# Turning the gathered rows of ten of eleven routed tiles by way of memory and VectorE's block transposes

## The chip, the core and the metric

The kernel runs on one core of a Trainium2 chip. The metric is the device time of one execution in microseconds (us), as the median of several runs. TensorE (PE in the profile), VectorE (DVE), ScalarE (ACT), GpSimd (POOL) and SyncE (SP) each work through their own instructions in order; SP here only issues DMAs.

## What is computed

The input is 625 rows of 1024 numbers and a graph of 20000 edges. A graph layer (normalise, per relation a projection and a mean over the edges, ELU, an output projection, a residual) gives x1. A mixture-of-experts layer follows, on h = layernorm(x1):

```python
sh = gelu(h @ sW1[s] + sb1[s]);  shared = mean_s(sh @ sW2[s] + sb2[s])
w  = softmax over the two largest of (h @ rW + rb), zero elsewhere
moe = sum_e w[:, e] * (gelu(h @ W1[e] + b1[e]) @ W2[e] + b2[e])      # 8 experts, 1024 -> 256 -> 1024
out = x1 + shared + moe
```

All of it is in float32. The change lies in the routed part, `gelu(h @ W1[e] + b1[e])` for the two experts that each row is routed to.

## The kernel before

**Order of the work.** A graph part, then the shared experts' first layer (`shared_in`, 32 groups of matmuls into p_sh), beside which VectorE works out the routing: which row sits in which slot of which tile (`tok`), and which expert each tile or part of a tile belongs to (`ej`, read into registers by TensorE and ScalarE). Then the routed first layer, the routed second layer (`p_yj`, whose rows are scattered to memory `yt`), the shared second layer (`p_o`) with the gathered sums, and the store.

**The routed tiles.** There are NJ = 11 tiles of 128 slots. Seven belong to one expert each, three are shared by two experts (64 slots each), one by four (32 each). Their order of work is the tuple `tiles`: 4, 5, 6, 0, 7, 1, 8, 2, 9, 10, 3. The text counts tiles in this order of work.

**The stages before the change.** `fetch` (L1368) gathers the tile's rows from memory `h2d` by an indirect DMA from GpSimd into `xs` (128 x 1024), of which there are three buffers in pool `io`; the bias rows `b2x` use the same three. TensorE then turns the rows: eight transposes of 128 x 128 into two PSUM banks (`p_x`, L1378), of which ScalarE copies the first to `xsT` (L1384) and VectorE the second (L1382). `xsT` has two buffers. `expert_in` (L1397) multiplies `xsT` with the expert's W1 into `p_h` (8 steps of 128 features), VectorE copies that to `hj` (L1401). `expert_mid` (L1409) turns `hj` by TensorE into `p_hT`, and ScalarE applies the GELU into `hjT` (L1412). The loop runs these three one step apart: fetch with turn of tile s, `expert_in` of s - 1, `expert_mid` of s - 2. For tiles with more than one expert, ScalarE copies the further experts' W1 to a fixed place (`w1m`, L1391), at set steps.

**What sets the order.** The program text is scheduled: each engine gets a fixed list of instructions, not always in the order of the text, and works through it in order. A DMA waits, in its engine's queue, for what it needs, and with it all behind it. SP's queue before the change, from the middle on: `yt` zeroed, W1 of two experts, both shared sW1, W1 of six experts, W2 of all eight experts (L1109, 1 MB each, into `w2a`), then (waiting for the last `p_h`) sW2 and the rows of x1, later the loads `g` from `yt` and the stores. `w2a` holds all eight experts' W2; the second layer picks from it by a register, so that its first matmul waits for all eight.

**Feature order.** W1 is loaded as `(k p) h -> p k h`: partition p holds features p, 128 + p, and so on, in runs of 1 KB, which fits the order in which the transposes lay the features out.

## Time and profile before

| | |
|---|---|
| median of 3 runs | 295.31 us (295.11 to 295.79) |
| the profiled execution | 294.8 us |
| its span, first to last instruction | 293.0 us |
| TensorE busy | 283.4 us (97%) |
| VectorE, ScalarE, GpSimd busy | 168.3, 103.2, 44.1 us |
| shared first layer ends | 161.1 us |
| routed first layer, first turn to first p_yj | 161.1 to 212.1 us |
| turns of the rows, p_x | 88 matmuls, 0.87 us for the eight of a tile |
| W1 loads issued | 94.0 to 129.9 us |
| W2 loads issued | 133.3 to 144.2 us |

The page has six parts: busy time by engine, the span in 40 slices, the DMA queues, the chain that ended last (followed back from the last instruction to whatever released each step), the costliest groups of instructions, and the DMA issues. Beside it stand answers of the trace: the chain in order of time, timelines of one engine (start, length, engine, line, operation, output and inputs, count, and in brackets the idle time before it with what ended it), and busy time by window. `PEld` is TensorE's loading of weights, and a name such as `ACTq` is an engine's queue, where register loads and waits are seen. A float32 matmul shows as two records, a transpose as one.

### The profile page before, as it was taken

Reading aid. Unit: us, or ns where it says so; the run is one execution under the profiler, and the core shown is the slowest. Engines: PE = TensorE matmul, PEld = TensorE weight load, DVE = VectorE, ACT = ScalarE, POOL = GpSimd, SP = SyncE. Lnnn points to the kernel's source line nnn. Section 1 sums busy time; section 2 is a strip of 40 time slices with the busy share of each in tenths; the row PEclk is TensorE's granted clock in tenths of the full one; section 3 lists DMA queues with packets and bytes.
Section 4 is the critical chain, followed back from the end, with each engine's and each line's share of the span. In section 5 each row is a group of like instructions: output and inputs, shape, how many; then the busy total and the mean of one; then the engine's idle time right before and its main releaser. Section 6 shows DMA issues by size and latency. Waiting matters only on the chain.

```text
span 293.0 us, 4532 instructions
## 1 busy us (share of the span) xinstructions
PE 283.4 (97%) x1573; PEld 192.1 (66%) x1573; DVE 168.3 (57%) x459; ACT 103.2 (35%) x237; POOL 44.1 (15%) x101
## 2 busy tenths in 40 slices
PE   7998999999999999899999999999999999999992
PEld 5876777778888555677777987778643334444451
DVE  5699999997874888746925322222134111157920
ACT  2348425513642323353105544656198111000000
POOL 9500000000000024420131312110012223200000
PEclk9999999999999999999999999999999999999998
DMA  6999930000000999999999742420095545389351
GB/s 229 344 322 408 408 117 2 2 1 2 0 0 4 327 364 392 393 392 369 409 353 408 283 143 78 140 74 0 2 342 230 211 194 226 136 332 403 134 156 53
DMA packets 28699, 61.41 MB, mean 210 GB/s; under 512 B 2150, under 2 KB 15981, under 8 KB 28666
## 3 DMA queue, kind: packets, MB, share of 16 engines
q1 hardware_dynamic: 23144, 44.17, 42.0%
q0 software_dynamic: 5232, 16.55, 15.4%
q10 hardware_dynamic: 296, 0.35, 0.5%
q8 instruction: 15, 0.25, 0.3%
q14 instruction: 12, 0.10, 0.1%
HBM read 43.02 MB, written 18.81 MB: 211 GB/s over the span
## 4 chain that ended last, share of the span: by engine, by line
PE 77%; DVE 20%; issue 1%; ACT 1%; ACTq 0%; DVEq 0%
PE p_h L1397 13%; PE p_yj L1455 13%; PE p_o L1510 12%; PE p_sh L1175 11%; PE p_pr L920 9%; PE p_agg L937 5%; PE p_x L1378 3%; DVE ohs L873 3%; DVE ohs L874 2%; PE p_y L983 2%; PE scrap L1000 2%; DVE xh L987 2%; DVE st L776 2%; DVE xh L807 1%; DVE ohk L877 1%; DVE h L747 1%
## 5 line engine op out<-in xcount | busy, mean ns | idle before, releaser
L920 PE MATMUL p_pr<-wg,nT 128*125 128x286 f32 x240 | 61.5, 409 | 1.0 <-ACT nT L825 0.8
L920 PEld LDWEIGHTS p_pr<-wg,nT 128*125 128x125 f32 x240 | 43.8, 187 | 13.2 <-ACT nT L825 1.8
L1397 PE MATMUL p_h<-w1a,xsT 128*128 (+2 forms) x176 | 40.0, 381 | 0.0
L1455 PE MATMUL p_yj<-w2a,hjT 128*128 (+2 forms) x88 | 38.6, 595 | 0.0
L1510 PE MATMUL p_o<-sw,shT 128*125 128x512 f32 (+1 forms) x88 | 36.1, 554 | 0.0
L1175 PE MATMUL p_sh<-h2T,sw 128*128 128x313 f32 (+1 forms) x128 | 35.2, 429 | 0.0
L1397 PEld LDWEIGHTS p_h<-w1a,xsT 128*128 128x128 f32 (+2 forms) x176 | 28.8, 169 | 7.4 <-issue 0.5
L1175 PEld LDWEIGHTS p_sh<-h2T,sw 128*128 128x128 f32 x128 | 23.7, 190 | 8.6 <-issue 0.2
L1455 PEld LDWEIGHTS p_yj<-w2a,hjT 128*128 128x128 f32 (+2 forms) x88 | 14.4, 169 | 22.4 <-issue 22.4
L1510 PEld LDWEIGHTS p_o<-sw,shT 128*125 128x125 f32 x88 | 16.4, 188 | 16.9 <-issue 16.2
L1459 DVE COPY ys<-p_yj 128x512 f32<-128x512 f32 x15 | 10.4, 692 | 28.7 <-PE p_yj L1455 27.0
L1401 DVE COPY hj<-p_h 128x256 f32<-128x256 f32 x11 | 4.7, 425 | 31.1 <-PE p_h L1397 31.1
L994 POOL DMA_DIRECT2D x1d<-xh x10 | 5.3, 531 | 92.4 <-DVE flagf L721 89.0
L983 PE MATMUL p_y<-wo_t,eT 128*125 128x512 f32 (+1 forms) x40 | 18.8, 592 | 0.0
L1463 POOL DMA_INDIRECT yt<-ys,row x11 | 10.8, 981 | 50.5 <-DVE ys L1459 50.5
L1412 ACT ACTIVATE hjT<-p_hT,vT 128x128 f32<-128x128 f32 (+2 forms) x34 | 8.7, 332 | 24.5 <-PE p_hT L1409 24.5
L1486 DVE SCALAR_TENSOR_TENSOR x<-p_o,x 125x512 f32<-125x512 f32 (+1 forms) x11 | 6.9, 639 | 16.3 <-PE p_o L1512 16.3
L1370 POOL DMA_INDIRECT xs<-h2d,tok x11 | 10.4, 948 | 34.5 <-PE p_x L1378 24.9
L937 PE MATMUL p_agg<-P,CT 125*125 125x288 f32 x100 | 15.5, 305 | 0.0
L1397 PE MATMUL p_h<-w1m,xsT 128*64 128x256 f32 (+1 forms) x96 | 14.7, 382 | 0.0
L1455 PE MATMUL p_yj<-w2m,hjT 128*64 128x512 f32 (+1 forms) x48 | 14.1, 595 | 0.0
L1382 DVE COPY xsT<-p_x 128x512 f32<-128x512 f32 x11 | 7.6, 692 | 11.0 <-PE p_x L1378 8.7
(309 smaller groups left out, 422.8 us busy)
## 6 DMA issues: line engine op xcount, KB each, us to landing
w1a<-in_L_ffn_W_dram SPq DMA_DIRECT2D x8, 1024.0 KB
w2a<-in_L_ffn_W_dram SPq DMA_DIRECT2D x8, 1024.0 KB
yt<-zero SPq DMA_DIRECT2D x2, 2560.0 KB
g<-yt SPq DMA_DIRECT2D x10, 512.0 KB
sw<-in_L_ffn_sW_dram SPq DMA_DIRECT2D x4, 1024.0 KB
x<-x1d SPq DMA_DIRECT2D x5, 500.0 KB
x1d<-xh POOLq DMA_DIRECT2D x5, 448.0 KB, 7.2
h2d<-h POOLq DMA_DIRECT2D x5, 448.0 KB, 6.8
```

Source lines behind the costliest of these rows:

```text
L873: nc.vector.tensor_tensor(os, row[:, None].to_broadcast(shape), key, op=ALU.is_equal)
L920: nc.tensor.matmul(p[:TP, :F], nT[:, k, m * TP : (m + 1) * TP], wg[:, k, r, :], start=(k == 0), stop=(k == KD - 1))
L937: nc.tensor.matmul(p[:TP, : F + 2], CT[:, m, at : at + TP], P[:, m, r, i], start=(m == 0 and i == 0), stop=(m == NT - 1 and i == 1))
L983: nc.tensor.matmul(ps[s][:TP, :], eT[:n, k, :], wo_t[:n, k, at], start=(k == 0), stop=False)
L1175: nc.tensor.matmul(p[:, : z - a], sw1[:, i, k, t * 128 : (t + 1) * 128], h2T[:, k, a:z], start=(k == 0), stop=(k == KD - 1))
L1370: nc.gpsimd.indirect_dma_start(out=xs, out_offset=None, in_=h2d, in_offset=bass.IndirectOffsetOnAxis(ap=tok[:, j : j + 1], axis=0))
L1378: nc.tensor.transpose(p[:, k * 128 : (k + 1) * 128], xs[:, at : at + 128], ident)
L1397: nc.tensor.matmul(p[a:b, :H], xsT[j][:, k, a:b], w1m[j, a][:, 0, k, :] if a else w1a[:, bass.ds(e, 1), k, :], start=(k == 0), stop=(k == ...
L1455: made = nc.tensor.matmul(p[a:b], hjT[:, j, k, a:b], w2m[j, a, k][:, at] if a else w2a[:, bass.ds(e, 1), k, at], start=(k == 0), stop=(k = ...
L1459: nc.vector.tensor_copy(y[:, at], p)
L1463: sent.append(nc.gpsimd.indirect_dma_start(out=yt, out_offset=bass.IndirectOffsetOnAxis(ap=row[:, j : j + 1], axis=0), in_=y, in_offset=No ...
L1510: nc.tensor.matmul(p[:TP, :n], shT[:, i, k, own], sw2[:, i, k, at], start=(i == 0 and k == 0), stop=False)
```

## The change

- Memory `xd` is added, 512 KB for each tile.
- For all tiles but the first, `fetch` also writes the gathered rows to `xd`, each row cut in four quarters of 256 features (a DMA on SP's queue).
- `turn` is one step later than the gather. For these ten tiles it reads `xd` back (again on SP's queue) such that partition 32b + r holds quarter b of rows 4r to 4r + 3. The landing place is one of two halves of the last expert's place in `w2a`. VectorE then turns blocks of 32 x 32 straight into `xsT`, in one instruction of 128 x 1024.
- The first tile is still turned by TensorE, taking every eighth column of `xs`.
- In `xsT`, partition p then holds features 8p to 8p + 7. So W1 is loaded as `(p k) h -> p k h`, one run of 8 KB for each partition.
- `w2a`: four experts are loaded where all eight were, three in the first steps of the loop, and the last one, into the landing place, after the last turn.
- `expert_in` and `expert_mid` come one step later, and the loop has one step more. The copies of `w1m` are ordered after the last GELU written ahead of them in place of the copy of `xsT`.

```diff
+    xd = dram.tile([NJ, 4, QC * D], F32, name="xd")
@@ load_w1
-            nc.sync.dma_start(w1a[:, e], W1[e].rearrange("(k p) h -> p k h", p=128))
+            nc.sync.dma_start(w1a[:, e], W1[e].rearrange("(p k) h -> p k h", p=128))
@@
-    for e in range(NE):
-        nc.sync.dma_start(w2a[:, e], W2[e].rearrange("(k p) d -> p k d", p=128))
+    def load_w2(es):
+        for e in es:
+            nc.sync.dma_start(w2a[:, e], W2[e].rearrange("(k p) d -> p k d", p=128))
+    load_w2(range(4))
@@ routed tiles
+    turned = [last_in]
+    fetched = {}
 
     def fetch(j):
         xs = io.tile([128, D], F32, tag="io", name=f"xs_{j}")
         nc.gpsimd.indirect_dma_start(
...
+        fetched[j] = xs
+        if j not in by_pe:
+            nc.sync.dma_start(xd[j].rearrange("b (n f) -> n b f", n=128), xs.rearrange("n (b f) -> n b f", b=4))
+
+    def through_blocks(s, t_):
+        j = tiles[s]
+        xq = w2a[:, NE - 1, s % HK].rearrange("p (a f) -> p a f", a=4)
+        nc.sync.dma_start(xq, xd[j].rearrange("b (r a f) -> (b r) a f", r=QC, a=4))
+        nc.vector.transpose(t_.rearrange("p k (r a) -> p a k r", a=4), xq.rearrange("p a (c k) -> p a k c", k=KD))
+
+    def turn(s):
+        j = tiles[s]
         t_ = xt.tile([128, KD, 128], F32, tag="xsT", name=f"xsT_{j}")
-        for g in range(2):
-            p = ps_acc(f"p_x{g}_{j}")
-            for k in range(4):
-                at = (4 * g + k) * 128
-                nc.tensor.transpose(p[:, k * 128 : (k + 1) * 128], xs[:, at : at + 128], ident)
...
+        if j in by_pe:
+            for g in range(2):
+                p = ps_acc(f"p_x{g}_{j}")
+                for k in range(4):
+                    nc.tensor.transpose(p[:, k * 128 : (k + 1) * 128], fetched[j][:, 4 * g + k :: KD], ident)
+                (nc.vector.tensor_copy if g else nc.scalar.copy)(
+                    t_[:, 4 * g : 4 * g + 4, :], p.rearrange("p (k n) -> p k n", k=4))
+        else:
+            through_blocks(s, t_)
         xsT[j] = t_
...
-            with tc.issue_after(copied.ins):
+            with tc.issue_after(turned[-1].ins):
@@ the loop
+    by_pe = [tiles[s] for s in (0,)]
-    for s in range(NJ + 2):
+    for s in range(NJ + 3):
         if s < NJ:
             fetch(tiles[s])
         if 0 <= s - 1 < NJ:
-            expert_in(tiles[s - 1])
+            turn(s - 1)
+        if 4 <= s + 4 - 1 < NE - 1 and s:
+            load_w2((s + 4 - 1,))
+        if s == NJ:
+            load_w2((NE - 1,))
         if 0 <= s - 2 < NJ:
-            expert_mid(tiles[s - 2])
+            expert_in(tiles[s - 2])
+        if 0 <= s - 3 < NJ:
+            expert_mid(tiles[s - 3])
```

More of the change, by code (lines that the diff above doesn't have):

```diff
@@ L1176, in shared_in @@
                                  h2T[:, k, a:z], start=(k == 0), stop=(k == KD - 1))
-            nc.scalar.activation(shT[:, i, t, a:z], p[:, : z - a], AF.Gelu, bias=vT[:, b : b + 1])
+            last = nc.scalar.activation(shT[:, i, t, a:z], p[:, : z - a], AF.Gelu, bias=vT[:, b : b + 1])
+        return last
     wab = const.tile([TP, 2, NT], F32, name="wab")
@@ L1345, in sparse_kernel @@
     for t in range(HK):
-        shared_in(1, t)
+        last_in = shared_in(1, t)
     sh_in.close()
@@ L1372, in fetch @@
             in_offset=bass.IndirectOffsetOnAxis(ap=tok[:, j : j + 1], axis=0))
-        t_ = xt.tile([128, KD, 128], F32, tag="xsT", name=f"xsT_{j}")
-        for g in range(2):
-            p = ps_acc(f"p_x{g}_{j}")
-            for k in range(4):
-                at = (4 * g + k) * 128
-                nc.tensor.transpose(p[:, k * 128 : (k + 1) * 128], xs[:, at : at + 128], ident)
-            o = t_[:, 4 * g : 4 * g + 4, :]
-            pv = p.rearrange("p (k n) -> p k n", k=4)
-            if g:
-                nc.vector.tensor_copy(o, pv)
-            else:
-                copied = nc.scalar.copy(o, pv)
+        fetched[j] = xs
[8 more added lines that the diff above has]
+        j = tiles[s]
+        t_ = xt.tile([128, KD, 128], F32, tag="xsT", name=f"xsT_{j}")
+        if j in by_pe:
[7 more added lines that the diff above has]
+            through_blocks(s, t_)
         xsT[j] = t_
@@ L1411, in expert_mid @@
             for a, b, e in parts(j):
-                nc.scalar.activation(hjT[:, j, t, a:b], p[:, t * 128 + a : t * 128 + b], AF.Gelu,
-                                     bias=bT[:, bass.ds(e, 1), t])
+                turned.append(nc.scalar.activation(hjT[:, j, t, a:b], p[:, t * 128 + a : t * 128 + b],
+                                                   AF.Gelu, bias=bT[:, bass.ds(e, 1), t]))
     whole = range(NM2, NJ)
```

## The prediction

> **What bounds the kernel now.** I read the page's busy shares first, then the chain that ended last around the changed stage, then the timelines of ScalarE and GpSimd there, then the DMA queues by window.

> ```profile
> PE 283.4 (97%) x1573; PEld 192.1 (66%) x1573; DVE 168.3 (57%) x459; ACT 103.2 (35%) x237; POOL 44.1 (15%) x101
> ```

> TensorE is the bound. In the routed stage the chain of work runs on TensorE alone:

> ```profile
> 161.14 1.75 PE p_x L1378 x16
> 162.88 3.46 PE p_h L1397 x16
> 166.34 0.87 PE p_x L1378 x8
> 167.21 3.46 PE p_h L1397 x16
> 170.67 0.22 PE p_hT L1409 x2
> 170.89 0.87 PE p_x L1378 x8
> ```

> Columns: start, length, work. Each tile pays 0.87 us for turning its rows (p_x) before 3.46 us of first-layer matmuls (p_h); the first two tiles' turns stand together. So work taken from TensorE here counts in full, if nothing later than TensorE comes up. The places where that can happen are the start and the end of the stage. At the start:

> ```profile
> 161.18 0.52 ACT L1177 ACTIVATE shT<-p_sh,vT 128x312 f32<-128x312 f32 x1 [1.68 <-PE p_sh L1175]
> 161.61 0.59 ACT L1384 COPY xsT<-p_x 128x512 f32<-128x512 f32 x1
> 162.54 0.59 ACT L1384 COPY xsT<-p_x 128x512 f32<-128x512 f32 x1 [0.34 <-PE p_x L1378]
> 164.39 2.18 ACT L1391 COPY w1m<-w1a 128x512 f32 x4 [1.26 <-DMA w2a<-in_L_ffn_W_dram]
> ```

> ```profile
> L1354 ACTq TENSOR_LOAD <-ej x1: 1452/1452/1452, 162.6 to 162.6; - x1
> ```

> ScalarE copies the first tiles' columns at once and only then does the register load and the four expert copies (w1m). The profile puts the wait of 1.26 us down to a DMA; the register load of 1.45 us in its queue fills that time better. The gathers:

> ```profile
> 147.18 1.04 POOL L1370 DMA_INDIRECT xs<-h2d,tok  x1 [0.32 <-DVE part L1330]
> 148.52 0.96 POOL L1370 DMA_INDIRECT xs<-h2d,tok  x1 [0.30 <-issue]
> 158.15 0.94 POOL L1370 DMA_INDIRECT xs<-h2d,tok  x1 [8.66 <-DVE b2h L645]
> ```

> By the DMA view these three land 8.6, 10.0 and 7.4 us after issue, because weight loads fill the engines until about 162.7; later ones take 4.1 to 5.2. The third gather waits for the b2h casts, which free its buffer.

> **What goes.** Ten of eleven turns leave TensorE. Nine of them stand behind the first p_h: 9 x 0.87 = 7.8 us off the chain. The tenth (0.87 us, beside the first) is counted in the start below. Their 20 copies from PSUM go too (0.59 us on ScalarE, 0.69 us on VectorE each); both engines have room there, so I count that at nothing.

> **What comes, in the steady part.** Per tile: a write of 512 KB to memory and a read back, both on SP's queue, and one VectorE block transpose of 128 x 1024. Of these the trace shows none. Nearest rows: for the read, the first g<-yt load (512 KB, issued 255.43), whose user starts at 259.15: 3.7 us. For the write I take about the same (the packets are 1 KB, see below). Gather 4.4, write 3.6, read 3.3 to 3.7 us follow one another, with three gather buffers and two landing halves. Stepping through SP's order with these numbers, every read lands before the tile two places earlier has left TensorE, or 1 to 2 us ahead of need: no wait. With write and read each 0.9 us slower, three tiles wait, 1.8 us in all.

> [...]

> **What moves, at the start.** The built order of instructions shows two moves that the diff does not. First, ScalarE's copy of the first tile's columns now stands behind the register load and the four w1m copies. From the last gelu: 161.2 + 1.45 + 0.34 (setup before the first copy, as now) + 2.18 = 165.2, copy 0.59, so the first p_h can start at 165.9 instead of 162.7. TensorE's own register load (1.56 us), now in front of the turn, and the turn's stride of eight elements lie inside that hole.

> Second, on VectorE the block transpose of tile two stands in front of the copy of tile one's second half. So the second half of the first p_h waits for the whole round trip of tile two. Stepped through:
> - The W1 loads get one long run per partition in place of eight of 1 KB. By windows, 95 to 100 us moved 1.52 MB in 1 KB packets at 93.6% of the engines (0.32 MB per us), 140 to 142 us 0.82 MB in 4 KB packets at 103% (0.40). So 8.4 MB take some 4 us less, and the first six W2 loads, in front of everything else in SP's queue, drain near 151 to 153.
> - Gather two (issued 148.5) lands near 155 instead of 158.5. SP, waiting for it, issues the write (lands about 158.7) and then the seventh W2 load.
> - Gather three still waits for b2h (now some 157.5) and lands near 162.2. Its write stands in front of the first read in SP's queue, so that read is issued at 162.7 although its data has been there since 158.7. Behind 512 KB of write it lands near 166.7.
> - Transpose 1.8, copy 0.69: 169.2. The second half of the first p_h (1.73) ends at 170.9. Now it ends at 166.2: **+4.7 us**. ScalarE alone would have made it 3.2.

> A hole of 3.9 us opens in TensorE (162.0 to 165.9); before, the longest in this region is 0.91. By the rows that show no change of rate after such a hole, nothing. [...] I count 0.2.

> **At the end.** The eighth W2 load must wait for the last transposes, whose landing place is its own. The last transpose starts when tile nine's p_h and copy are done (+0.42), ends 1.8 later, and the load (1 MB at 0.41 MB per us, 2.6, plus some 2.3 that the 512 KB load shows beside its bytes) lands about 7.2 us after that p_h. The second layer needs it 7.85 us after (now from 203.40 to 212.12, less one turn of 0.87). [...] Behind the load in SP's queue stand the sw2 and x1 loads, which wait for p_h anyway.

> **Sum.** -7.8 + 4.7 + 0.2 = -2.9 us. The profiled execution took 294.8 (span 293.0 and 1.8 around it), which would become 291.9; it lies 0.5 below the median of 295.31, so on the median's scale 292.4.

> **Rivals.**
> 1. The start is cheaper: gathers and first read land by 164, so that only ScalarE's order counts. -7.8 + 3.2 = -4.6: 290.7. For it: the read needs only the write of 158.7. Against: SP's order puts the third gather before it. 0.15.
> 2. The gain is eaten at the start: the third gather takes 7.4 us as now, and the write and read are slower. Each microsecond of later landing adds one. +2.9 us: 295.3, no change. It counts from a first read landing after about 169. 0.20.
> 3. [...] 0.07.
> 4. The forecast itself, 290.0 to 294.5: 0.58.

> **Numbers.** A measurement of this kernel can tell about 0.2% (0.6 us) from no change. Cases 1 and 4 are faster but for a small part of 4; case 2 splits into same and slower, with some steady waits. Faster 0.74, same 0.10, slower 0.16. Range 289.8 to 296.5: down to a start without any wait of VectorE, up to case 2 with one slow round trip more; case 3 is left out.

> **What would show it.** In the changed profile: p_x x8 only; ScalarE's w1m copies ahead of its xsT copy, and a TensorE hole of 3 to 4 us near 162; the VectorE row of the transpose between 1.2 and 2.4 us; the wait before the second half of the first p_h put down to VectorE or the xd read; from the second tile on a period of about 3.7 us with no gap; the eighth W2 load landing before the first p_yj. Wrong: if the transpose is above 3 us, if VectorE's waits on reads come back at each tile, or if the first read lands after 169.

## The result and the profile after

The changed kernel takes 309.49 us (median of 4 runs, 307.19 to 310.31), the kernel before 295.21 beside it (294.77 to 295.79): a ratio of 1.047, 95% interval 1.041 to 1.053. It is slower, by 14.3 us, where 2.9 less was forecast, and the time lies outside the range. A run more than 1.5% above the fastest of its kernel counts as slow and is left out of the ratios here, though not of the median times; three of the four runs of early read are slow (all but 304.94 us), and so are the profiled runs of early read and of four in order. The profiled execution of after took 307.19 us with a span of 305.4, so 12.4 more than the profiled one of before.

First the page of after: busy time, and the granted clock of TensorE in 40 slices of 7.6 us.

```profile
PE 278.5 (91%) x1493; PEld 185.0 (61%) x1493; DVE 181.4 (59%) x459; ACT 98.1 (32%) x227; POOL 44.2 (14%) x101
...
PEclk9999999999999999999996599889999999999998
```

TensorE has 80 instructions less (ten turns of eight), as meant. But its share fell from 97% to 91%, and in the slices from 160.3 to 176 us (6 and 5 tenths) and from 191 to 206 us (8 and 8) TensorE is not granted its full clock. Below is the timeline of TensorE in after, only the rows with a wait ahead of them: start, length, work, and in brackets the idle time and who ended it.

```profile
163.98 3.78 PE L1415 MATMUL p_h<-w1a,xsT 128*128 x8 [3.73 <-ACT xsT L1399]
...
173.03 6.97 PE L1415 MATMUL p_h<-w1a,xsT 128*128 x24 [5.26 <-DVE xsT L1399]
...
188.36 3.69 PE L1415 MATMUL p_h<-w1a,xsT 128*128 x16 [0.49 <-DVE xsT L1389]
...
195.73 0.40 PE L1415 MATMUL p_h<-w1a,xsT 128*64 x1 [3.46 <-DVE xsT L1389]
...
207.16 0.40 PE L1415 MATMUL p_h<-w1a,xsT 128*64 x1 [2.02 <-DVE xsT L1389]
```

Five holes, 14.96 us together, where before had none. From the first p_x to the first p_yj, the stage, before took 50.99 us and after 63.40: the whole 12.4. The sum: 50.99 - 8.7 (ten turns at 0.87) + 14.96 (holes) = 57.25. Another 5 us is the half clock behind the holes, read from the same rows: eight matmuls in 3.78 us (1.99 in two of the runs further down), 24 in 6.97 where 24 x 0.216 + 0.16 = 5.3 is usual, and the tile at 195.73 some 1.6 longer than its usual 3.6. The last 1.1 us no single row shows.

What the holes wait for is in the chain of waits of after (start, length, what):

```profile
157.04 7.60 DMA xs<-h2d,tok
...
164.66 3.23 DMA xd<-xs
...
169.88 5.84 DMA xs<-h2d,tok
...
175.73 6.66 DMA xd<-xs
...
184.37 5.73 DMA xs<-h2d,tok
...
190.58 6.61 DMA w2a<-xd
...
197.28 1.70 DVE xsT L1389
198.98 5.86 DMA w2a<-xd
```

Before, this stretch of the chain was TensorE alone. Now it is gather, write, read, one behind another, and from 170 us on each takes 5.7 to 6.7 us where the prediction reckoned 4.4, 3.6 and 3.3 to 3.7. The windows show what has changed: the first line is before, the others are after. Columns: window, its length, busy time of each engine with instructions, granted clock, busy share of the 16 DMA engines, GB/s.

```profile
177.00:181.00 4.00, 4.00 (x39) 2.82 (x36) 0.52 (x2) 0.68 (x3) 0.52 (x1) 1.00 0.48 137
```

```profile
169.00:173.00 4.00, 0.00 (x0) 0.00 (x0) 2.61 (x2) 0.00 (x0) 2.17 (x3) 0.50 1.05 407
173.00:177.00 4.00, 3.97 (x11) 3.28 (x12) 0.35 (x2) 0.00 (x0) 0.28 (x1) 0.61 0.96 323
177.00:181.00 4.00, 4.00 (x21) 3.49 (x21) 2.65 (x4) 0.74 (x3) 0.87 (x1) 1.00 1.05 362
...
189.00:193.00 4.00, 3.27 (x17) 2.62 (x15) 0.00 (x0) 2.29 (x8) 0.77 (x1) 1.00 1.04 350
193.00:197.00 4.00, 1.27 (x10) 1.02 (x12) 2.36 (x2) 2.29 (x6) 0.17 (x1) 0.95 1.02 373
197.00:201.00 4.00, 4.00 (x24) 2.64 (x20) 2.08 (x1) 0.00 (x0) 0.00 (x0) 0.62 0.45 143
...
157.00:209.00 52.00, 37.03 (x192) 28.22 (x192) 19.36 (x16) 17.16 (x40) 8.45 (x9) 0.84 0.87 298
```

The DMA engines, half idle before, are nearly full from 161 to 197 us (a share of 0.85 to 1.05). By the last line they are busy for 45.3 us (0.87 of 52) between 157 and 209 us and move 15.5 MB in that time (298 GB/s), so 0.34 MB per us. Three transfers of 0.52 MB, the gather, write and read of a tile, are then **4.6 us of all 16 engines for a tile, against 3.7 to 3.9 us of TensorE** (3.7 for a tile of one expert, 3.9 for a shared one). The expectations below, written before this was summed so, reckon 4.2 to 4.3.

The last hole (2.02 us) has another history. From 197 to 199 us the DMA engines move next to nothing (a share of 0.21 and 0.00 in windows of 1 us): in SP's queue the read that TensorE then lacks, issued at 198.98, stands behind the last tile's write, issued at 198.50, which had waited for the last gather. That is the chain's doing, not the bytes'.

Two steps of the forecast as they came out, from the timelines of ScalarE and VectorE:

```profile
161.27 2.17 ACT L1409 COPY w1m<-w1a 128x512 f32 x4 [1.34 <-issue]
163.36 0.57 ACT L1399 COPY xsT<-p_x 128x512 f32<-128x512 f32 x1
```

```profile
170.36 2.06 DVE L1389 STREAM_TRANSPOSE xsT<-w2a 128x1024 f32<-128x1024 f32 x1 [13.59 <-DMA w2a<-xd]
```

The w1m copies do stand ahead of the xsT copy, and the first read landed at 170.3, not 166.7.

### The profile page after: what moved, and what is told of

Read it like the earlier page. It is cut to its first block, busy times and chain, and to the rows that moved or that the text cites. A ratio compares the mean times of both kernels' runs of the same rounds, so it can differ in the third digit from the quotient of the medians.

```text
span 305.4 us, 4389 instructions
## 1 busy us (share of the span) xinstructions
PE 278.5 (91%) x1493; PEld 185.0 (61%) x1493; DVE 181.4 (59%) x459; ACT 98.1 (32%) x227; POOL 44.2 (14%) x101
## 3 DMA queue, kind: packets, MB, share of 16 engines
q0 software_dynamic: 5232, 16.55, 14.3%
## 4 chain that ended last, share of the span: by engine, by line
PE 49%; DVE 20%; DMA 19%; issue 7%; SPq 1%; POOL 1%; ACT 1%; POOLq 0%; DVEq 0%; ACTq 0%
PE p_yj L1480 13%; PE p_o L1535 11%; PE p_pr L921 9%; DMA xs<-h2d,tok 6%; PE p_h L1415 5%; PE p_agg L938 5%; DMA w2a<-xd 4%; DMA xh<-in_x_dram 3%; DMA xd<-xs 3%; DMA b2x<-bd 2%; DVE ohs L874 2%; DVE ohs L875 2%; PE p_y L984 2%; DVE xh L988 2%; PE p_sh L1180 1%
## 5 line engine op out<-in xcount | busy, mean ns | idle before, releaser
L1415 PE MATMUL p_h<-w1a,xsT 128*128 (+2 forms) x176 | 45.2, 415 | 15.0 <-DVE xsT L1389 6.0
L1415 PEld LDWEIGHTS p_h<-w1a,xsT 128*128 128x128 f32 (+2 forms) x176 | 31.6, 185 | 24.3 <-issue 6.9
L1389 DVE STREAM_TRANSPOSE xsT<-w2a 128x1024 f32<-128x1024 f32 x10 | 21.0, 2098 | 25.8 <-DMA w2a<-xd 25.8
L1535 PEld LDWEIGHTS p_o<-sw,shT 128*125 128x125 f32 x88 | 16.4, 187 | 16.9 <-issue 16.2
L1415 PE MATMUL p_h<-w1m,xsT 128*64 128x256 f32 (+1 forms) x96 | 16.3, 403 | 0.0
L1378 POOL DMA_INDIRECT xs<-h2d,tok x11 | 10.5, 950 | 37.6 <-DMA xd<-xs 27.1
L938 PE MATMUL p_agg<-P,CT 125*125 125x288 f32 x100 | 15.5, 304 | 0.0
L875 DVE TENSOR_TENSOR ohs<-ohs,cols 125x1024 f16<-125x1024 f16 (+1 forms) x22 | 13.8, 628 | 0.0
```

Source lines behind the costliest of these rows:

```text
L875: last = nc.vector.tensor_tensor(os, os, both(VV_, 128)[1], op=ALU.mult)
L938: nc.tensor.matmul(p[:TP, : F + 2], CT[:, m, at : at + TP], P[:, m, r, i], start=(m == 0 and i == 0), stop=(m == NT - 1 and i == 1))
L1378: nc.gpsimd.indirect_dma_start(out=xs, out_offset=None, in_=h2d, in_offset=bass.IndirectOffsetOnAxis(ap=tok[:, j : j + 1], axis=0))
L1389: nc.vector.transpose(t_.rearrange("p k (r a) -> p a k r", a=4), xq.rearrange("p a (c k) -> p a k c", k=KD))
L1415: nc.tensor.matmul(p[a:b, :H], xsT[j][:, k, a:b], w1m[j, a][:, 0, k, :] if a else w1a[:, bass.ds(e, 1), k, :], start=(k == 0), stop=(k == ...
L1535: nc.tensor.matmul(p[:TP, :n], shT[:, i, k, own], sw2[:, i, k, at], start=(i == 0 and k == 0), stop=False)
```

## The experiments

Theory B: the DMA engines' throughput bounds the stage. Rival A: the links (a chain of gather, write and read through three buffers and queues in order), whatever the bytes. Contributor C: the half clock behind the holes. Ratios are to the kernel before, measured beside it. "Stage" and "holes" are read from each profile as above, so each is of one run, which need not lie near the median (five in order: 292.92 us, the fastest of twelve).

| kernel | by memory | time us | ratio, 95% interval | stage | holes |
|---|---|---|---|---|---|
| before | 0 | 294.5 to 295.2 | 1 | 50.99 | 0 |
| after | 10 | 309.49 | 1.047, 1.041 to 1.053 | 63.40 | 14.96 |
| all by TensorE | 0 | 299.14 | 1.0155, 1.0108 to 1.0201 | 57.29 | 2.82 |
| ... with filler | 0 | 298.05 | 1.0123, 1.0079 to 1.0168 | 54.22 | 1.92 |
| ... with ScalarE's old order | 0 | 294.57 | 0.9993, 0.9968 to 1.0019 | 51.34 | 0 |
| half bytes | 10 | 303.51 | 1.0292, 1.0235 to 1.0349 | 61.81 | 11.58 |
| half bytes, 4 buffers | 10 | 299.13 | 1.0165, 1.0116 to 1.0213 | 55.49 | 10.73 |
| early read | 10 | 309.96 | - | 63.84 | 15.81 |
| no links | 10 | 307.66 | 1.0436, 1.0373 to 1.0499 | 63.75 | 14.73 |
| no write | 10 | 294.28 | 0.9986, 0.9962 to 1.0011 | 48.58 | 4.26 |
| first tile early | 10 | 307.81 | 1.0431, 1.0394 to 1.0468 | 62.33 | 15.59 |
| long packets | 10 | 307.58 | 1.0435, 1.0382 to 1.0488 | 61.57 | 14.22 |
| alternate | 5 | 297.34 | 1.0087, 1.0044 to 1.013 | 52.89 | 5.11 |
| five, own buffers | 5 | 302.98 | 1.0288, 1.0261 to 1.0314 | 59.31 | 9.25 |
| five, in order | 5 | 295.75 | 1.0053, 1.0026 to 1.0081 | 50.79 | 3.11 |
| four | 4 | 297.03 | 1.0047, 1.0011 to 1.0084 | 53.68 | 5.11 |
| four, own buffers | 4 | 303.95 | 1.0321, 1.029 to 1.0352 | 59.93 | 9.92 |
| four, in order | 4 | 297.36 | 1.0078, 1.0046 to 1.0109 | 52.14 | 3.57 |
| three, spaced | 3 | 294.95 | 1.0032, 1.0006 to 1.0059 | 52.65 | 2.33 |
| two, spaced | 2 | 292.98 | **0.9937, 0.9913 to 0.9962** | 49.36 | 0 |

### Throughput or links

**Early read.** The read no longer waits for its tile's write.

```
-        nc.sync.dma_start(xq, xd[j].rearrange("b (r a f) -> (b r) a f", r=QC, a=4))
+        nc.sync.dma_start(xq, h2d[:128].rearrange("n (a f) -> n a f", a=4))
```

> All bytes are still moved, but the read takes 128 plain rows of h2d in place of the tile's own (the routed data is that of other rows), so it no longer waits for its tile's write. Theory A (the chain of waits): with this link gone the waits go, 291 to 297 us. Theory B (throughput): gather, write and read still need about 4.3 us of the DMA engines per tile, some 43 us for the ten from about 157 us on; TensorE still waits for 8 us or more in all: 302 to 309 us.

Four runs, 304.94 to 310.17 us, all far above the 291 to 297 of theory A: this link alone is not what the kernel loses by. Whether it is worth nothing or some 4 us the spread leaves open. The chain of the profiled run (309.87 us) shows gather and write waiting for each other:

```profile
162.50 5.29 DMA xs<-h2d,tok
...
167.81 6.62 DMA xd<-xs
...
175.16 4.68 DMA xs<-h2d,tok
...
179.86 6.72 DMA xd<-xs
```

That left the link between gather and write as a form of theory A, so it was to be cut too.

**No links.** The early read, and a write from the W1 tile.

```
-            nc.sync.dma_start(xd[j].rearrange("b (n f) -> n b f", n=128), xs.rearrange("n (b f) -> n b f", b=4))
+            nc.sync.dma_start(xd[j].rearrange("b (n f) -> n b f", n=128), w1a[:, 0, :4])
```

> All the bytes of the round trips are still moved, with packets of the same sizes, but nothing waits for anything: the write takes a part of the W1 tile in place of the gathered rows, the read takes plain rows of h2d (the routed tiles' data is that of other rows). Theory A (the chain gather, write, read with three buffers, of which the half-byte run showed a period of some 11.8 us for three tiles): all waits in the steady part go; only the start's ScalarE order and a half clock after it stay: 292 to 297 us. Theory B (throughput): gather, write and read still take 4.2 us of all DMA engines per tile and the three late W2 loads 2.6 each; even started earlier they can't keep up with 3.7 us per tile: 300 to 308 us.

307.66 us, the number that theory B forecast, with 14.73 us of holes. But the run does not show what it was meant to. Here are SP's queue and, from the chain, the first read:

```profile
109.34 35.59 SPq L1383 DMA_DIRECT2D xd<-w1a  x7
145.36 5.12 SPq L1112 DMA_DIRECT2D w2a<-in_L_ffn_W_dram  x5
150.53 2.46 SPq L1388 DMA_DIRECT2D w2a<-h2d  x1
```

```profile
150.53 23.53 DMA w2a<-h2d
```

Writes that wait for nothing go out long before the stage, eight of the ten by 145 us, and the W2 loads, which stand behind them in SP's queue, are issued from 145.36 us on (in the changed kernel six of them from 134.39 us on, within 3.2 us). So what fills the engines from 153 to 185 us, at a share of 1.02 to 1.06, is above all displaced W2 loads with gathers and reads, and a read that waits for no write takes 23.5 us. From 197 us on, with that worked off, the share is 0.10 to 0.44 and no hole is left. So full engines alone can hold TensorE up, with no link to blame; what the links cost in the changed kernel it leaves open.

**No write.** The read from h2d, and no write.

```
-            nc.sync.dma_start(xd[j].rearrange("b (n f) -> n b f", n=128), xs.rearrange("n (b f) -> n b f", b=4))
```

> The write is left out; the read takes plain rows of h2d in place of the tile's own (the routed tiles' data is that of other rows). Gather and read are left: 1 MB, 2.8 us of all DMA engines per tile against 3.7 us of TensorE. Theory B: no waits in the steady part; of the start, ScalarE's order (3.1 us) and perhaps a half clock (3.2 us) stay: 290 to 295 us. If the block transposes on VectorE or the reads alone were what delays: 300 us or more.

294.28 us, as theory B said: the holes behind the start are 0.55 us in all, though ten block transposes and ten reads are there. So neither VectorE's transposes nor the reads alone delay. Without a write a gather buffer is free at once, so this run takes away bytes and links together. Even so its median only equals the kernel before: the start hole (3.71 us) and a half clock behind it eat most of the gain (the profiled run, 292.88 us, has a stage 2.4 us shorter).

**Half bytes.** Write and read carry two of the four quarters, with all waits; two half transposes take the place of one.

```
+            nc.sync.dma_start(xd[j].rearrange("b (n f) -> n b f", n=128), xs.rearrange("n (b f) -> n b f", b=4)[:, :2])
+        nc.sync.dma_start(xq[:, :2], xd[j].rearrange("b (q a f) -> (b q) a f", q=64, a=2))
```

> Write and read of each tile carry half the bytes, with every wait kept as it is; VectorE turns the same half twice, so half of each routed tile's columns hold the other half's data. Theory B (DMA throughput: 4.3 us of all 16 engines per tile against 3.7 us of TensorE): some 2.9 us per tile now, so the waits behind the second tile vanish and the first two (3.7 and 5.3 us) shrink by about half, and the half clock after them mostly goes: 293 to 299 us. Theory A (the serial chain gather, write, read with three buffers and one queue in order, whose latency hardly depends on the bytes): waits of 2 to 5 us stay at most of the same places, 303 to 308 us.

303.51 us: on the edge of what theory A said, not what B said. The traffic fits now (a share of 0.61 to 0.94 from 165 to 193 us), but a hole of 5.48 us stays in the steady part. GpSimd's timeline shows three gathers together at 168.9 to 171.6 and again at 180.7 to 183.2: a gather (4.45 us), its write (6.63) and 0.7 on GpSimd before the buffer is used again, 11.8 us for three tiles or 3.9 a tile, which is at or over TensorE's 3.7 to 3.9. A second limit, then, that lies close behind the first. To test it:

**Half bytes, four buffers.** A fourth gather buffer in the unused half of the landing place; gathers held in order.

```
+        xs = io.tile([128, D], F32, tag=f"io{s % 4}", name=f"xs_{j}") if s % 4 != 3 else w2a[:, NE - 1, 1]
+        with tc.issue_after(got[-1].ins):
```

> The half-byte kernel (303.5 us; half of each routed tile's columns hold the other half's data) with a fourth gather buffer, in the half of the landing place that it doesn't use, and the gathers held in order. Theory of two limits: a cycle of gather and write takes 11.8 us there; with four buffers in place of three that is 3.0 us per tile, under TensorE's 3.7, so the wait of 5.5 us in the steady part goes, with the half clock behind it (2.4 us): 295 to 299 us. If buffers don't matter: 302 to 305 us.

299.13 us, just above what was expected, and the hole of 5.48 is 0.36. So at half the bytes the cycle of the buffers, or the order of the gathers, which was changed with it, is the second limit. The start got worse (6.66 us for 2.38), since four gathers now run before the first read.

**Long packets.** The write goes out in whole rows.

```
+            nc.sync.dma_start(xd[j].rearrange("b (n f) -> (b n) f", f=D), xs)
```

> The changed kernel with the same bytes and waits, but each tile's write goes out in whole rows, in packets of 4 KB in place of 1 KB (the tile's columns then come back in another order). Estimate from the windows of before (0.40 MB per us in 4 KB packets, 0.32 to 0.34 in 1 KB): some 0.3 us of the DMA engines less per tile. Theory B (throughput): up to 3 us less for ten tiles: 305 to 308 us. Theory A (links and latency): no change, 308 to 311 us.

307.58 us: in the direction of theory B and inside its numbers, but its interval overlaps that of the changed kernel; alone it settles nothing.

**Taken together.** Half bytes and no write move the same bytes, 1 MB a tile in place of 1.5. With the links that is 303.51 us (299.13 with a fourth buffer), without them 294.28: at that size the links cost up to 9.2 us. (Half bytes keeps half a write, no write none, so the kinds of transfer differ.) At the full bytes no run separates the two, and none puts the reads on another queue than the writes, so what SP's order adds stays untested.

What the bytes cost by themselves can be estimated from the changed kernel's trace. From 157 us on, 29 transfers of 0.52 MB and a W2 load of 1.05 MB are left, 16.2 MB, which at 0.34 MB per us last until about 204.5 us. With the last tile's transpose (2.1 us) and matmuls (3.9) the stage would then be some 51 us long: as long as before, where the forecast needed 48. So by this estimate the bytes alone take the whole gain. The other 12 us lie in how the transfers follow one another (by 197 us the engines have moved nine gathers and nine writes, but only six reads), in the start and in the half clock (5 us); how these divide is not shown.

### The start and the clock

**All by TensorE.** W1's layout, the later W2 loads, the extra step and ScalarE's order stay.

```
-    by_pe = [tiles[s] for s in (0,)]
+    by_pe = [tiles[s] for s in range(NJ)]
```

> All eleven tiles are turned by TensorE; the W1 layout, the later W2 loads, the extra step of the loop and ScalarE's new order stay. Every theory that puts the loss on the round trip through memory (too much traffic for the DMA engines, or its chain of waits) expects the time of before, plus at most the 3.2 us that ScalarE's order was reckoned at: 295 to 298 us, no wait of TensorE over 1 us behind the first p_h. If the rest of the change (layout, order of loads) is what costs, it stays above 304 us.

299.14 us, more than expected: 4.4 us of the loss have nothing to do with the round trip. By its windows (columns as above):

```profile
161.00:163.00 2.00, 0.03 (x1) 0.00 (x0) 0.69 (x1) 1.86 (x4) 1.28 (x2) 1.00 1.03 371
163.00:165.00 2.00, 1.15 (x3) 0.98 (x4) 0.00 (x0) 1.28 (x3) 0.00 (x0) 0.56 0.89 352
165.00:167.00 2.00, 2.00 (x7) 1.55 (x6) 0.00 (x0) 0.00 (x0) 0.00 (x0) 0.50 0.30 119
```

The hole of 2.82 us that ScalarE's order opens is followed by half clock (0.50), and the first p_h takes 6.78 us for its usual 3.62: 3.2 more. Hole and half clock are 6.0 of the 6.3 us by which the stage is longer.

**Filler.** The same with eight more transposes of the second tile's rows, which repeat what stands there (24 p_x at the start in place of 16).

```
-                for k in range(4):
+                for k in range(12 if s == 1 and g else 4):
```

> All tiles turned by TensorE as in the first experiment (299.1 us there), but the second group of the first tiles' turns is followed by 8 more transposes for each of two groups' places that repeat what stands there, so that TensorE works on through most of the 2.8 us hole before the first p_h, whose end ScalarE sets. Theory C (that hole drops TensorE to half clock for 6.8 us, worth 3.2 us in that profile): the granted clock stays at 1.00 and the time falls by about 3 us to 295.5 to 297 us. If the half clock is not what costs: no change, 298 to 300 us.

The profile shows a clock of 1.00 throughout and a first p_h of 3.72 us, and the stage is 3.1 us shorter, which is theory C's amount. The timed median fell by 1.1 us only and the intervals overlap. By the granted clock of each timed run, three of the four of all by TensorE have the 0.987 of the profiled one (299.11 to 300.88 us), the fourth 0.996, and that one took 298.30. So the half clock comes in most of its timed runs; whether it costs them 3.2 us or nearer 0.8 is not settled.

**ScalarE's old order.** All by TensorE, and the w1m copies queued behind the latest xsT copy.

```
+                if not g:
+                    turned.append(c)
```

> All tiles turned by TensorE as in the first experiment, but the w1m copies are put behind the latest xsT copy on ScalarE, as in the kernel before. If ScalarE's order (3.1 us of hole) and the half clock that follows it (3.2 us) are all that separates that kernel from the one before: no hole, 294 to 296 us, equal to before within 0.3%. If the W1 layout, the strided turn or the later W2 loads cost something by themselves: 297 us or more.

294.57 us, equal to before. So W1's layout, the later W2 loads, the extra step and the strided turn cost nothing; the order does.

**First tile early.** In the changed kernel both copies of the first tile on ScalarE, ahead of w1m.

```
-                (nc.vector.tensor_copy if g else nc.scalar.copy)(
-                    t_[:, 4 * g : 4 * g + 4, :], p.rearrange("p (k n) -> p k n", k=4))
+                turned.append(nc.scalar.copy(
+                    t_[:, 4 * g : 4 * g + 4, :], p.rearrange("p (k n) -> p k n", k=4)))
```

> The changed kernel with both column copies of the first tile on ScalarE and ahead of the w1m copies, so that neither ScalarE's order nor the block transpose on VectorE delays the first p_h (which was complete only 9 us after it could have been). Theory B (throughput): the reads of the other tiles land when they did, the end of the stage is set by the last of them, and later waits grow by what the first ones shrink: 306 to 310 us. If the start is what makes the loss (orders on ScalarE and VectorE, the first half-clock stretch): 3.5 to 6 us are won, 303.5 to 306 us.

307.81 us, what theory B said: the first p_h is done at 166.0 rather than 176.6, and the next hole is 8.51 us in place of 5.26. What the start gives, the later waits take.

### How many tiles may go this way

**Alternate** (steps 2, 4, 6, 8 and 10 by memory) and **four** (2, 4, 6, 8, ScalarE's old order, the eighth W2 load a step earlier).

```
+    by_pe = [tiles[s] for s in (0, 1, 3, 5, 7, 9)]
+    by_pe = [tiles[s] for s in (0, 1, 3, 5, 7, 9, 10)]
```

> Only every second tile (five of them, the third tile first) goes through memory, the others are turned by TensorE. Theory B: two tiles need two gathers, one write and one read, some 5.7 us of the DMA engines against 7.8 us of TensorE: no waits in the steady part; 5 x 0.87 = 4.4 us saved less up to 3.2 us of ScalarE's order at the start: 291 to 295 us. Theory A: each tile that goes through memory still waits for its chain, 2 us and more five times: 298 to 304 us.

> Four tiles go by memory (steps 2, 4, 6 and 8), seven by TensorE, with the w1m copies behind the xsT copies on ScalarE and the eighth W2 load issued one step earlier. Theory B with the start repaired: two tiles need 5.7 us of DMA engines against some 7.8 us of TensorE, no waits: 4 x 0.87 = 3.5 us saved: 291 to 292.5 us, faster than before. Theory A: each of the four waits for its chain by 1 to 2 us: 293 to 297 us.

297.34 and 297.03 us, both a little slower than before and slower than theory B alone would have it. In the chain of the four-tile kernel:

```profile
176.91 4.99 DMA xs<-h2d,tok
...
181.92 3.27 DMA xd<-xs
...
185.93 5.68 DMA xs<-h2d,tok
```

From gather to gather 9.0 us for two tiles (9.3 the next time), while TensorE needs 8.8 for them, one turn included (175.57 to 185.59 us less a hole of 1.25; the expectations reckoned 7.8): a gather waits until the write has left the buffer. So the buffers' cycle, the second limit, would explain the later holes (0.15 and 0.68 us); the next runs put it to the test.

**Four and five, own buffers.** The gathers of the memory tiles land in the eighth W2 expert's place, the reads in a place of their own.

```
+        xs = (io.tile([128, D], F32, tag="io", name=f"xs_{j}") if j in by_pe else w2a[:, NE - 1, s // 2 % HK])
+        xq = io.tile([128, D], F32, tag="land", bufs=1, name=f"xq_{j}").rearrange("p (a f) -> p a f", a=4)
```

> Four tiles by memory as in the run before (297.0 us there), but their gathered rows land in the two halves of the eighth W2 expert's place, what is read back lands in a place of its own, and the seven others share two gather buffers: no gather waits for a write that has only just gone out. Theory of two limits (DMA throughput for ten tiles; for four, the cycle of gather and write through shared buffers, seen there as 9.0 us per two tiles against 7.8 us of TensorE): the waits of 3.0, 1.3, 0.2 and 0.7 us go, and 4 x 0.87 = 3.5 us are saved: 290.5 to 292 us, faster than before. If throughput alone decides even for four tiles (some 6 us of DMA engines per two tiles): the waits stay, 294 to 297 us.

> The same with the last tile by memory too (five in all), and the eighth W2 load after the last read is issued, since the last two gathers' writes leave its place earlier than a block transpose would. Theory of two limits: 5 x 0.87 = 4.4 us saved, less up to 1 us of waiting for the eighth W2 load ahead of the second layer: 290 to 292 us. Throughput alone: 294 to 298 us.

303.95 and 302.98 us, above both forecasts. The separate buffers changed the order of the gathers: GpSimd issues two later memory tiles' gathers, which wait 12.2 and 6.3 us for writes (12.8 and 6.5 with five), ahead of the fourth tile's, and TensorE waits 7.99 (8.88) us for that one. With the order held:

```
+        with tc.issue_after(got[-1].ins):
+            got.append(nc.gpsimd.indirect_dma_start(
```

> Four tiles by memory with their own gather buffers, as in the run that took 304.0 us, but the gathers are issued in the order of the tiles. Theory: the 8.0 us wait there was the fourth tile's gather, queued on GpSimd behind two gathers that waited for a write; in order it goes, and with separate buffers the waits of the shared-buffer version (297.0) go too: 290.5 to 293 us, faster than before. Otherwise (waits stay for another reason): 295 to 300 us.

> Five tiles by memory, gathers in order, as above: 5 x 0.87 = 4.4 us saved, less up to 1 us at the eighth W2 load: 290 to 293 us. Otherwise: 295 to 300 us.

297.36 and 295.75 us: the long wait is gone, four holes of 0.5 to 1.5 us remain in each (3.57 and 3.11 in all), and there is no gain. So buffers of their own did not bring it, and what the waits of four and five tiles come from stays open. In the chain of the five-tile kernel two of its reads take 7.03 us each, among gathers that GpSimd issues two and three at a time.

**Three and two, spaced.** Steps 3, 6 and 9; steps 4 and 8; shared buffers, gathers in order, ScalarE's old order.

```
+    by_pe = [tiles[s] for s in range(NJ) if s not in (3, 6, 9)]
+    by_pe = [tiles[s] for s in range(NJ) if s not in (4, 8)]
```

> Three tiles by memory (steps 3, 6 and 9), the rest by TensorE, ScalarE's order as before, gathers in order. A round trip (gather 5, write 3, read 3.5 to 7, transpose 2.1 us) has some 17 us of TensorE work between the freeing of its buffer and its use. If the waits come from too short a time for the round trip and from traffic: none left, 3 x 0.87 = 2.6 us saved: 291.5 to 293 us, faster than before. If each round trip costs what it saves (contention with the other gathers): 294 to 296 us, no gain.

> The same with two tiles by memory (steps 4 and 8). Waits gone: 2 x 0.87 = 1.7 us saved, 292.5 to 293.5 us. If each round trip costs what it saves: 294 to 296 us.

Three: 294.95 us. Only the first of them waits (2.33 us), but the clock halves behind it (0.61 in 177 to 181 us) and that tile's p_h takes 5.36 for 3.6; hole and half clock eat 4.1 us. Two: 292.98 us, no hole at all, 1.6 us off the stage for the 1.7 expected, a ratio of 0.9937 to the kernel before: a gain of 1.5 us, small but clear of the noise, and faster than both kernels.

## Why the prediction was wrong

- **The step that failed: "every read lands before the tile two places earlier has left TensorE, or 1 to 2 us ahead of need: no wait."** It stepped each transfer through with the duration that it has in a half idle system, and never added up what three transfers of 512 KB per tile ask of the DMA engines: 4.6 us against 3.7 to 3.9 of TensorE. The windows were at hand (before: a share of 0.42 to 0.48 there, with about one gather per tile), and three times that is over 1. Its own trial with 0.9 us more per transfer gave 1.8 us of waiting; write and read took up to 6.7 us for its 3.6, and the steady part's three holes are 5.97 us, with no half clock counted. Shown: the engines are full while TensorE waits, the bytes alone need a stage as long as before (the estimate above), and with the write gone, bytes and links, so is the loss (294.28 us). Not shown: how the rest of the loss divides between the bytes and the links, which cost up to 9.2 us at 1 MB a tile; the last hole, 2.02 us, comes from the links.
- **The start, +4.7.** ScalarE's order came as said (xsT copy at 163.36, after the w1m copies; a hole of 3.73 us). Gather three was issued at 157.04, as said, but took 7.60 us for 4.7, its write went out at 164.66, and the first read landed at 170.3 for 166.7: the engines are full from the first tile on (a share of 0.99 from 161 to 165 us); the two holes are 8.99 us. The text's own bound ("after about 169 the gain is gone") was passed. The size was off; yet with the start repaired the time hardly moves, so this term was not what decided.
- **The clock, +0.2**, for a lower rate behind the hole at the start. No run shows this term. The half clock cost about 5 us in the profile, and likely as much in each timed run, since all four have its mean granted clock (0.966 to 0.970, the profiled one 0.967). One hole was reckoned with; there are five, and the clock falls at two of them and stays low through a third. Nor does the length of a hole alone decide: in the all-TensorE run a hole of 2.82 us was enough, the grant falling some 2.2 us after the last matmul and staying low for some 6.8 (read from the grant of 1-us windows), while in the alternate run a hole of 2.80 us left it at 1.00. The last section has the working.
- **The turns, -7.8, and the tenth.** Right: ten turns are gone.
- **The block transpose, 1.8.** No run shows this term: the ten transposes of the changed kernel took 2.06 to 2.18 us each. Of the rows of before, VectorE's f32 tensor_tensor of 96 x 1024 (L648), which walks without gaps, took 1.22. That the steps of 32 bytes in the transpose's source are the reason is not shown: no run here has another step. VectorE is not the bound: with the ten transposes and no write, the holes behind the start are 0.55 us in all.
- **The eighth W2 load.** Right: no wait before the first p_yj here (in the alternate run TensorE does wait 1.00 us for it).
- **W1's layout and the moved W2 loads at nothing.** Right, by the run with ScalarE's old order.
- **The rivals.** Rival 2 named the start alone and stopped at no change. The case that happened, DMA engines as the bound, was not among them.

What stays open: how the loss divides between bytes and links, and whether ten tiles with more gather buffers would do better (no run has a fourth full one; by the estimate above it could at best come back to the time before). The 1.1 us left over in the sum was not traced to rows.

## What to carry to other kernels

Before a turn is moved from TensorE to a trip through memory, add up the busy time of all DMA engines per tile, old transfers too, at the rate that the windows show, and compare it with the engine that sets the pace; durations of single transfers from an idle stretch say nothing of it (here 3.6 us were reckoned for a write that took up to 6.7). Then reckon the cycle of a buffer (gather, write, reuse) the same way: at 1 MB a tile the links still cost up to 9.2 us. A part of the tiles may be worth moving where all are not: here two of eleven.

## What the hardware showed that was not expected

```profile
159.09:162.50 3.41, 1.17 (x10) 0.90 (x8) 0.00 (x0) 1.75 (x4) 0.94 (x1) 1.00 0.99 334
...
193.22:196.63 3.41, 0.90 (x9) 0.76 (x11) 2.36 (x2) 2.07 (x5) 0.00 (x0) 1.00 1.04 378
...
203.46:206.87 3.41, 1.67 (x9) 1.22 (x7) 1.94 (x1) 1.70 (x6) 0.00 (x0) 1.00 0.29 112
```

  Cut on the grid that their own falls give, the traces of before and after have 160 windows that kept the full clock, busy for 1.67 us or more, and four ahead of a fall (two of them at the program's end), busy for 1.17 or less. In eleven other runs the clock falls within the stage, 18 times, which places the grid to some 0.05 us: each time TensorE had been busy for 1.2 us or less, and the least busy window that kept the full clock had some 1.45 (first tile early, 164.6 to 168.0 us). In all twelve stages it came back behind windows busy for 3.12 us or more and stayed at half behind 2.82 or less. The two holes of 2.8 us fit: all by TensorE had a window busy for 1.18 us (159.85 to 163.26); that of alternate (162.48 to 165.28) fits if it is spread over two, which is not shown, since no fall in its stage places the grid. So in these traces a hole halves the clock if it covers some 2.0 to 2.2 us of one window. An estimate from these figures (3.41 less 1.45 or 1.2): a hole of 1.9 us does not do it, one of 2.8 does in half to two thirds of its positions, the 3.9 of the prediction in more than four of five.
- A 512 KB write on nearly idle engines (issued 160.65 in the four-tile kernel, the DMA share 0.00 from 160.5 to 161.5 us) had moved its bytes by some 163.3 (a share of 0.35 from 163.0 to 163.5, 0.03 or less from there to 165.5), yet counted as landed only at 165.5; later ones took 2.9 to 3.3 us from issue to landing.
